# A four-layer graph network on one core: two VectorE operations read PSUM, one block changes from multiplying to gathering, one group of steps is timed by the count alone

## The chip, the cores and the metric

The kernel runs on one core of a Trainium2 chip. The metric is the device time of one execution in microseconds; of several executions the median is given, with the lowest and the highest. The engines are called as the profile calls them: PE (TensorE matmul), PEld (its weight load), DVE (VectorE), ACT (ScalarE), POOL (GpSimd) and SP (SyncE, which here issues DMAs only).

## The reference, cut to what matters

There are 6250 nodes with 256 channels each and 100,000 edges, sorted by destination. Each of four layers adds to every node the sum of the rows of its sources and sends the result through three small matrix products; the fourth layer is the head, whose middle width is 64.

```python
def agg(h):
    return jax.ops.segment_sum(h[src], dst, num_segments=N)
for l in range(NL - 1):
    h = x + agg(x)
    h = jax.nn.relu(h @ W1s[l] + b1s[l])
    h = jax.nn.relu(h @ W2s[l] + b2s[l])
    x = h @ W3s[l] + b3s[l]
h = x + agg(x)
h = jax.nn.relu(h @ cW1 + cb1)
h = jax.nn.relu(h @ cW2 + cb2)
return h @ cW3 + cb3
# called with h = max(layernorm(x), 0); the result is added to x
```

Everything is float32. The layer norm and the last addition to x are a small part of the time.

## The kernel before, in words

**Blocks.** The nodes are cut into 49 blocks of 128 destinations. The rows of all nodes stay in SBUF as a tile `XY` of 128 x 49 x 512: for each block 256 channels of a rounded high part and 256 of the rest, so that two fast passes make a float32 product. The same rows lie in DRAM as `table0` to `table3`, one per layer.

**Two ways to aggregate.** A destination block is either multiplied or gathered.

- Multiplied: a matrix of edge counts, 128 destinations against all 6250 sources, is multiplied with `XY`. That is 49 matmuls named `agg`: line 1797 in layer 0, where the block's counts have just been built, and line 1880 in layers 1 to 3 for groups of four blocks (line 1797 again for a block that stands alone). The counts themselves are built in layer 0 by matmuls named `bp` (line 1202) from one-hots named `hi` and `lo` (DVE, line 1164), cast to bytes (lines 1210 and 1212) and written to DRAM for the later layers.
- Gathered: POOL issues 16 indirect DMAs (sometimes one more, named `over`), each bringing the rows of 128 edges from the table (line 1557). PE then adds them into one PSUM tile `sums` with narrow one-hot matrices `hot` (23 matmuls, 46 records in the profile, line 1620). This is called a visit. `hot` is made by DVE on line 1601 by comparing the column numbers `colf` with the destinations `rel`. DVE then adds the block's own rows: `u` from the two halves of `XY` (line 1641, issued at once after the visit's matmuls), and three steps later `u + sums` (line 1650).

**After the aggregation** both ways go on alike: transposes (line 1681, named a turn), a relu into `h1`, then what the code calls seconds (line 1379: the second matrix product) and thirds (line 1442: the third; in the head lines 1371 and 1391, with line 1439 for a piece of the end). Their outputs become the next layer's `XY` and table. A block's old rows in `XY` may be overwritten once all uses are marked in a set named `used`.

**Which block goes which way.** Layer 0 gathers 24 blocks (0 to 18 and 44 to 48) and multiplies 25 (19 to 43; block 19 comes first, alone). Layers 1, 2 and 3 gather 21, 20 and 19 and multiply the rest.

**The order of the work** is written out when the program is built, by a planner that counts two things: `now`, one tick for each unit of (usually) four `agg` matmuls, and `clock`, an estimate of PE's time. `Gathered.flow` sends gathers at an even pace over a layer by the estimate; each gather is tied to the PE matmul after which it was sent (`after(...)`, which becomes a semaphore wait on POOL). `Gathered.meets` says when a visit is due: when the estimate has reached it, or a fixed number of ticks before the layer's end (`LATE`), and not sooner than four ticks after the visit before. A visit that is due sends whatever of its gathers is not yet sent. Turns wait in a list `jobs`, seconds and thirds in a list `queue`, each with a first and a last tick; between the two they are placed at the next visit, and at the last tick at any rate (the stretch is `SPAN`, six ticks). `step` (line 1262 on) keeps the entries of `queue` a few ticks apart (`free`). The group of the last gathered block of a layer, block 48, is marked `hurry` and has no such stretch; the group gathered just before it (44 to 47 in layer 0, blocks from 16 on in later layers) has one like all the others.

Of the kernel before, what the change touches and what calls it, by code (L numbers as in the profile page):

```python
# [8 lines left out]
F32 = mybir.dt.float32  # L9
# [5 lines left out]
OP = mybir.AluOpType  # L15
PSUM = bass.MemoryType.PSUM
DRAM = bass.MemoryType.DRAM
P = 128
# [378 lines left out]
def sorted_edges(  # L397
# [38 lines left out]
    nc = tc.nc  # L436
    N, C = x.shape
# [16 lines left out]
    Q = P // 4  # L454
    T = 16
# [14 lines left out]
    gone = [(0, 4), (4, 4), (8, 4), (12, 4), (16, 4), (44, 4), (48, 1)]  # L470
    panels = [(20, 4), (24, 4), (28, 4), (32, 4), (36, 4), (40, 4), (44, 4)]
    solos = [[], [], [19], [18, 19]]
# [2 lines left out]
    S0 = 2 * min(place_of)  # L475


    teams = [(19, 1), (20, 4), (24, 4), (28, 4), (32, 4), (36, 4), (40, 2), (42, 2)]
    made = [b + i for b, n in teams for i in range(n)]
    for i in range(panels[-1][1]):  # L480
        made.insert((4, 9, 14, 18)[i], panels[-1][0] + i)
    made.insert(23, 18)
    assert sorted(made) == sorted(place_of) and sum(gone[-3]) == panels[0][0] and gone[-2] == panels[-1] and all(n == gone[0][1] for _, n in gone[:-1]) and sorted(
        b + i for b, n in gone[:-2] + gone[-1:] + panels for i in range(n)) == list(range(NT))
    NQ = len(gone)
# [2 lines left out]
    left = [T * sum(n for _, n in gone[:q]) for q in range(NQ + 1)]  # L488
# [15 lines left out]
    XY = const.tile([P, NT, 2 * C], F32R, name="XY")  # L504
# [581 lines left out]
    with tc.manual_schedule():  # L1086
# [167 lines left out]
        def step(visit):  # L1254

            g = queue[0]
            rush = any(o["hurry"] for o in queue)
            first, last = g["first"], g["last"]
            if rush:
                first = min(first, g["since"] + 3)  # L1260
            if now[0] < max(first, free[0]) or not (visit or last <= now[0] or rush):
                return
            g["steps"].pop(0)()
            lock[0] = now[0] + (1 if g["hurry"] else 2)
            free[0] = now[0] + (2 if g["hurry"] else 3 if rush else 4)
            g["since"] = now[0]
            if g["steps"]:
                g["first"], g["last"] = now[0] + g["far"], now[0] + g["far"] + SPAN
            else:
                queue.pop(0)  # L1270

# [30 lines left out]
        def reload(l, j):  # L1302

            if (l, j) in used and (l, j) in kept and l < NLAYER:
                wanted.append((l, j))
                bring()
# [39 lines left out]

            later(2, biased)

        def mlp(l, b0, n, h1, hurry, far):

            w = n * P
            end = l == NLAYER
# [124 lines left out]
            def thirds():  # L1477
# [4 lines left out]
                for i in range(0, n, 2):  # L1482
                    third(i)

            wait = 1 if hurry else far - 2
            queue.append(dict(steps=[seconds, thirds], since=now[0], first=now[0] + wait,
                              last=now[0] + wait + (0 if hurry else SPAN),
                              far=2 if hurry else far, hurry=hurry))


        class Gathered:
            def __init__(self, l):
                self.l, self.sent, self.done = l, 0, 0
                self.first, self.rest, self.turns = None, 0, []
                b0, n0 = teams[0] if l == 0 else panels[-1]
                others = solos[l] + [b0 + i for i in range(n0)]
                self.blocks = [(b, n if l or b != gone[-3][0] else n - teams[0][1], i,
                                left[q] + i * T)
                               for q, (b, n) in enumerate(gone) for i in range(n)
                               if b + i not in others]  # L1500
                self.alone = {b + i for b, n, i, _ in self.blocks}
                self.visits = [(g, rounds) for g in range(len(self.blocks)) for rounds in ROUNDS]
                self.n = len(self.visits)
                self.rows, self.us, self.hots = {}, [], -1

                self.order, self.upto, self.shared = [], [0], {}
                seen_over = set()
                for g, rounds in self.visits:
                    b = self.blocks[g][0] + self.blocks[g][2]
                    new = [T] if over_of[b] not in seen_over else []  # L1510
                    seen_over.add(over_of[b])
                    used_at = {k: i for i, c in reversed([*enumerate(rounds)])
                               for k in range(c, T + 1, 4) if k in (*range(own[b]), *new)}
# [70 lines left out]
            def one_hots(self, v):  # L1584
                if self.hots >= v:
                    return
                self.hots = v
                g, rounds = self.visits[v]
                which = over_of[self.blocks[g][0] + self.blocks[g][2]]
                if which not in known:  # L1590
                    known.add(which)
                    m = P // Q - 1
                    c = T - 4 * m - min(rounds)
                    for b in over[which]:
                        nc.vector.tensor_scalar(
                            rel[:, list(own).index(b), 0, c, m:m + 1],
                            late_dst[:, which:which + 1], float(-b * P), None,
                            op0=OP.add)
                shape = [P, len(rounds), P // Q, Q]
                self.hot = work.tile(shape, F32, name="hot")  # L1600
                nc.vector.tensor_tensor(
                    self.hot,
                    colf.rearrange("p (m q) -> p m q", q=Q)[:, None, :, :].to_broadcast(shape),
                    rel[:, self.blocks[g][3] // T, v % len(ROUNDS), :, :, None].to_broadcast(shape),
                    OP.is_equal)

# [31 lines left out]
            def finish(self, b, n, g, sums):  # L1638
                u = work.tile([P, C], F32, name="u", bufs=2)
                self.us.append(u)  # L1640
                nc.vector.tensor_tensor(u, XY[:, b + g, :C].bitcast(F32),
                                        XY[:, b + g, C:].bitcast(F32), OP.add)
                used.add((self.l, b + g, 0))
                if (self.l, b + g, 1) in used:
                    used.add((self.l, b + g))
                    reload(self.l, b + g)
                behind = []
                later(1, lambda: behind.extend(paced))
                later(1 if b == gone[-1][0] else 3, lambda: after(
                    nc.vector.tensor_tensor(u, u, sums[:, :C], OP.add),  # L1650
                    "a full product stands behind the sums", behind))

                self.closed(b, n, g)

            def closed(self, b, n, g):
                if g % 2 or g == n - 1:
                    us, self.us = self.us, []

                    def turn():
                        if g < 2:  # L1660
                            self.h1 = work.tile([P, KC, W], F32, name="h1", bufs=2)
                        turned(self.l, us, self.h1, g)
                        if g == n - 1:
                            mlp(self.l, b, n, self.h1, b == gone[-1][0], far)

                    far = FAR - 2 if b == self.blocks[-2][0] else FAR
                    if b == gone[-1][0]:
                        later(2, turn)
                    else:
                        job(far - 2, far - 2 + SPAN, turn)  # L1670
                        self.turns.append(jobs[-1])
                if g + 1 < n and (self.l, b + g + 1) in alone:
                    self.us.append(alone.pop((self.l, b + g + 1)))
                    self.closed(b, n, g + 1)
# [31 lines left out]
        alone = {}  # L1706
        spare = clT.rearrange("p a q s -> p (a q s)").bitcast(F32)
        sums = ps_g.tile([P, W], F32, name="sums")
        MARGIN = 6.0
        TAIL = [16.0] + [-5.0] * (NLAYER - 1) + [-3.0]  # L1710
        LATE = [-8] + [10] * (NLAYER - 1) + [-5]
# [294 lines left out]
```

## Time and profile before

| | |
|---|---|
| median of 3 runs | 2053.34 us (2052.33 to 2054.1) |
| profiled execution | 2053.2 us, its span 2051.3 us, granted clock 0.994 |
| PE busy | 1997.9 us, 97% of the span |
| POOL busy | 1416.9 us, 69%; 1336 `rows` gathers of 0.991 us on average |
| DVE, ACT busy | 45%, 42% |
| preparation before layer 0's products | to about 105 us |
| layer 0, 1, 2, 3 (with the end) | to about 661, 1155, 1619, 2051 us |

The profiled execution spends 1.9 us outside its span. A row of the groups reads: line, engine, operation, output and inputs, how often; then busy time and mean duration, and the engine's idle time just before, with what ended it. A row of the timeline reads: start, duration, engine, line, operation, and in brackets the idle time before it and its releaser.

### The profile page before, as it was taken

To read this page: it belongs to the slowest core of one execution; us is meant where nothing else is said; L and a number is where in the kernel's file an instruction comes from. 1 tells how busy PE (TensorE), PEld (TensorE's weight loads), DVE (VectorE), ACT (ScalarE), POOL (GpSimd) and SP (SyncE) were. 2 spreads that over 40 slices of the span, in tenths; PEclk is the share of its full clock that TensorE was granted. 3 is DMA by queue.
4 is the path that set the end of the run, shared out by engine and by line. 5 is a ranking of instruction groups with operands and counts; after the bars stand their busy time and mean duration, and the time that the engine had idled before them with its cause. 6 is when DMAs were issued, how large, how long until landed. Compare 5 with 4: busy or idle time off the path is not lost.

```text
span 2051.3 us, 33099 instructions
## 1 busy us (share of the span) xinstructions
PE 1997.9 (97%) x12078; PEld 1480.8 (72%) x12078; DVE 912.8 (45%) x2093; ACT 853.5 (42%) x1746; POOL 1416.9 (69%) x1460
## 2 busy tenths in 40 slices
PE   6999999999999999999999999999999999999997
PEld 5767666666767777777777777777777777777675
DVE  6888776676662422222334322222234332333333
ACT  5776655555555533322233433323334433323231
POOL 4657777777774477777777377777777277777773
PEclk9999999999999999999999999999999999999999
DMA  6544555454455655555556554455456455665554
GB/s 198 163 137 151 156 148 160 152 155 151 147 158 172 213 165 156 156 178 156 167 171 205 172 162 151 148 171 174 140 180 212 147 183 167 202 195 190 175 155 129
DMA packets 182290, 341.84 MB, mean 167 GB/s; under 512 B 31588, under 2 KB 117108, under 8 KB 182118
## 3 DMA queue, kind: packets, MB, share of 16 engines
q0 software_dynamic: 67376, 181.01, 30.0%
q1 hardware_dynamic: 112566, 156.54, 23.2%
q10 hardware_dynamic: 2176, 2.10, 0.3%
q8 instruction: 96, 1.57, 0.3%
q14 instruction: 76, 0.62, 0.1%
HBM read 282.26 MB, written 57.26 MB: 166 GB/s over the span
## 4 chain that ended last, share of the span: by engine, by line
PE 90%; DVE 3%; DMA 3%; issue 1%; ACT 1%; POOL 1%; SPq 0%; DVEq 0%; ACTq 0%; POOLq 0%
PE agg L1880 46%; PE agg L1797 14%; PE sums L1620 10%; PE ps L1442 6%; PE ps L1379 6%; PE bp L1202 4%; DMA rows<-table,idx 2%; PE ps L1681 1%; DVE hi L1164 1%; DVE at L1212 1%; PE ps L1391 1%; DVE lo L1164 1%; PE ps L1371 0%; PE bp L1030 0%; DMA wd<-in_dst_dram,starts 0%
## 5 line engine op out<-in xcount | busy, mean ns | idle before, releaser
L1557 POOL DMA_INDIRECT rows<-table,idx x1336 | 1323.6, 991 | 559.5 <-issue 227.1
L1880 PE MATMUL agg<-a,XY 128*128 128x512 f32 x4116 | 977.9, 395 | 2.0 <-ACT a L1773 2.0
L1880 PEld LDWEIGHTS agg<-a,XY 128*128 128x128 f32 x4116 | 766.0, 188 | 190.9 <-issue 33.0
L1773 ACT CAST a<-at 128x512 fp32r<-128x512 uint8 (+1 forms) x536 | 325.3, 618 | 622.5 <-PE agg L1880 591.7
L1773 DVE CAST a<-at 128x512 fp32r<-128x512 uint8 x535 | 243.9, 458 | 498.1 <-PE agg L1880 471.5
L1797 PE MATMUL agg<-XY,a 128*128 128x512 f32 x1372 | 380.9, 410 | 1.4 <-ACT a L1757 0.7
L1797 PEld LDWEIGHTS agg<-XY,a 128*128 128x128 f32 x1372 | 241.1, 190 | 44.6 <-issue 5.4
L1620 PE MATMUL sums<-rows,hot 128*32 128x256 f32 x3680 | 240.7, 381 | 9.8 <-DMA rows<-table,idx 9.7
L1620 PEld LDWEIGHTS sums<-rows,hot 128*32 128x32 f32 x3680 | 121.6, 110 | 122.9 <-issue 31.5
L1210 ACT CAST at<-bp 128x392 uint8<-128x392 f32 x250 | 121.0, 489 | 197.0 <-PE bp L1202 196.4
L1757 ACT CAST a<-at 128x512 fp32r<-128x512 uint8 (+2 forms) x349 | 190.7, 575 | 6.6 <-PE agg L1797 6.2
L1212 DVE CAST at<-bp 128x392 uint8<-128x392 f32 x230 | 129.4, 563 | 137.0 <-PE bp L1202 136.7
L1650 DVE TENSOR_TENSOR u<-u,sums 128x256 f32<-128x256 f32 x84 | 35.2, 420 | 282.1 <-PE agg L1880 265.1
L1164 DVE TENSOR_TENSOR hi<-cols,pairs 128x784 bf16<-128x784 bf16 x240 | 134.5, 561 | 0.0
L1442 PE MATMUL ps<-w,h 128*128 128x256 f32 x588 | 133.6, 379 | 0.9 <-ACT h L1382 0.9
L1379 PE MATMUL ps<-h,w 128*128 128x512 f32 (+3 forms) x328 | 133.1, 548 | 0.3 <-ACT h L1893 0.3
L1202 PE MATMUL bp<-hi,lo 128*128 128x196 bf16 x960 | 125.9, 252 | 6.3 <-DVE hi L1164 5.7
L1202 PEld LDWEIGHTS <-lo 128*128 128x128 bf16 x960 | 70.9, 98 | 75.1 <-issue 26.0
L1442 PEld LDWEIGHTS ps<-w,h 128*128 128x128 f32 x588 | 111.5, 190 | 17.6 <-ACT h L1382 1.3
L1164 DVE TENSOR_TENSOR lo<-lanes,pairs 128x512 bf16<-128x512 bf16 x240 | 99.9, 416 | 2.7 <-ACT pairs L1159 1.5
L1379 PEld LDWEIGHTS ps<-h,w 128*128 128x128 f32 x328 | 60.0, 190 | 53.9 <-issue 42.9
L1450 DVE TENSOR_TENSOR zz<-ps,w 128x512 f32<-128x512 f32 (+1 forms) x76 | 50.3, 672 | 107.4 <-PE ps L1442 107.4
(214 smaller groups left out, 1041.6 us busy)
## 6 DMA issues: line engine op xcount, KB each, us to landing
at<-mat SPq DMA_DIRECT2D x150, 448.0 KB
mat<-at SPq DMA_DIRECT2D x30, 784.0 KB
rows<-table,idx POOLq DMA_INDIRECT x1336
table<-zz SPq DMA_DIRECT2D x71, 256.0 KB
back<-table SPq DMA_DIRECT2D x95, 128.0 KB
xs<-in_x_dram SPq DMA_DIRECT2D x8, 768.0 KB
table<-zs SPq DMA_DIRECT2D x12, 512.0 KB
out_dram<-zz SPq DMA_DIRECT2D x23, 256.0 KB
```

The costliest lines, as they stand in the source:

```text
L1164: nc.vector.tensor_tensor(o.rearrange("p q (n t) -> p q n t", t=2), values.rearrange("p (n t) -> p n t", t=2)[:, None, :, :].to_broadcast( ...
L1202: mm = nc.tensor.matmul(bp[:, m * HW:(m + 1) * HW], lo[:, q + m, :], hi[:, q + m, :], start=True, stop=True)
L1210: nc.scalar.copy(o, v)
L1212: nc.vector.tensor_copy(o, v)
L1379: mm = nc.tensor.matmul(ps[:mp, :w], weights[l][0][:, c, i * P:i * P + mp], h1[:, c, :w], start=(c == 0), stop=(c == KC - 1))
L1442: mm = nc.tensor.matmul(o, h2[0][:, c, nodes], w3[:, c, :], start=(c == 0), stop=(c == KC - 1))
L1557: got = nc.gpsimd.indirect_dma_start(out=t, out_offset=None, in_=tables[self.l][:, :], in_offset=bass.IndirectOffsetOnAxis(ap=at, axis=0),)
L1620: nc.tensor.matmul(self.sums[m * Q:(m + 1) * Q, :C], self.hot[:, c - min(rounds), m, :], self.shared[over_of[b + i]] if k == T else self.r ...
L1757: nc.scalar.copy(a[:, i * m * P:(i + 1) * m * P].rearrange("p (j d) -> p j d", j=m), counts[b][:, j:j + m, :])
L1773: cast(o, at[:, :, d:d + m * P])
L1797: mm = nc.tensor.matmul(agg, a[:, d:d + P], XY[:, j, :], start=(j == 0), stop=(j == NT - 1))
L1880: mm = nc.tensor.matmul(agg[c][:, :w], XY[:, j, o:o + P], a[:, :w], start=(at == 0 and half == 0), stop=(at == NT - 1 and half == 1))
```

## The change

Three things are changed together.

1. **PSUM operands.** `colf` is copied once into a part of the PSUM tile `sums` that the visits do not use, and the comparison that makes `hot` reads it there. The own rows are added in two steps that each read one operand in PSUM: first the low half of `XY` onto `sums` in place, then `sums` plus the high half into `u`. Both now come after the visit, where before only the second did, and the mark in `used` moves to the second.
2. **The group before the last.** It is marked `brisk`: its turn is placed four ticks after its visit, seconds two ticks later, thirds three ticks after those, without a stretch. `step` keeps two ticks after a step while a `hurry` group is queued (three before), and three after a brisk one (four before).
3. **25 and 24.** In layer 0 block 19 is now gathered, in the group of 16 to 19. Its counts are still built, since layers 2 and 3 use them, but as the 26th block instead of the first.

```diff
-    teams = [(19, 1), (20, 4), (24, 4), (28, 4), (32, 4), (36, 4), (40, 2), (42, 2)]
+    teams = [(20, 4), (24, 4), (28, 4), (32, 4), (36, 4), (40, 2), (42, 2)]
...
-    made.insert(23, 18)
+    for i, b in ((23, 18), (25, 19)):
+        made.insert(i, b)
...
-            free[0] = now[0] + (2 if g["hurry"] else 3 if rush else 4)
+            free[0] = now[0] + (2 if g["hurry"] or rush else 3 if g["brisk"] else 4)
             g["since"] = now[0]
             if g["steps"]:
-                g["first"], g["last"] = now[0] + g["far"], now[0] + g["far"] + SPAN
+                g["first"], g["last"] = now[0] + g["far"], now[0] + g["far"] + (0 if g["brisk"] else SPAN)
...
-            wait = 1 if hurry else far - 2
+            wait = 1 if hurry else 2 if brisk else far - 2
             queue.append(dict(steps=[seconds, thirds], since=now[0], first=now[0] + wait,
-                              last=now[0] + wait + (0 if hurry else SPAN),
-                              far=2 if hurry else far, hurry=hurry))
+                              last=now[0] + wait + (0 if hurry or brisk else SPAN),
+                              far=2 if hurry else far, hurry=hurry, brisk=brisk))
...
-                    colf.rearrange("p (m q) -> p m q", q=Q)[:, None, :, :].to_broadcast(shape),
+                    sums[:, C:C + P].rearrange("p (m q) -> p m q", q=Q)[:, None, :, :].to_broadcast(shape),
...
-                nc.vector.tensor_tensor(u, XY[:, b + g, :C].bitcast(F32),
-                                        XY[:, b + g, C:].bitcast(F32), OP.add)
-                used.add((self.l, b + g, 0))
-                if (self.l, b + g, 1) in used:
-                    used.add((self.l, b + g))
-                    reload(self.l, b + g)
                 behind = []
+
+                def whole():
+                    after(nc.vector.tensor_tensor(sums[:, :C], sums[:, :C],
+                                                  XY[:, b + g, C:].bitcast(F32), OP.add),
+                          "a full product stands behind the sums", behind)
+                    nc.vector.tensor_tensor(u, sums[:, :C], XY[:, b + g, :C].bitcast(F32), OP.add)
+                    used.add((self.l, b + g, 0))
+                    if (self.l, b + g, 1) in used:
+                        used.add((self.l, b + g))
+                        reload(self.l, b + g)
+
                 later(1, lambda: behind.extend(paced))
-                later(1 if b == gone[-1][0] else 3, lambda: after(
-                    nc.vector.tensor_tensor(u, u, sums[:, :C], OP.add),
-                    "a full product stands behind the sums", behind))
+                later(1 if b == gone[-1][0] else 3, whole)
...
-                    far = FAR - 2 if b == self.blocks[-2][0] else FAR
+                    brisk = b == self.blocks[-2][0]
+                    far = 3 if brisk else FAR
...
-                        job(far - 2, far - 2 + SPAN, turn)
+                        wait = 4 if brisk else far - 2
+                        job(wait, wait + (0 if brisk else SPAN), turn)
...
         sums = ps_g.tile([P, W], F32, name="sums")
+        nc.vector.tensor_copy(sums[:, C:C + P], colf)
```

Over the whole program PE has 49 `agg` matmuls of layer 0 fewer and 23 `sums` matmuls more; POOL has 16 rows more; the stretches of `agg` matmuls begin 30 times fewer right after `bp` matmuls (200 instead of 230). In the changed file line 1797 is 1803, 1880 is 1886, 1681 is 1686, 1442 is 1443, 1379 is 1380, 1371 is 1372 and 1391 is 1392. The rest of the order is mostly the old one. Three places where it moves follow.

**PE where layer 0 ends and layer 1 begins.** `agg<-XY,a` is layer 0's product, `agg<-a,XY` layer 1's, `ps<-w,h` are thirds and `ps<-h,w` seconds of gathered groups. Before:

```order
L1442 MATMUL ps<-w_1185,h_8205 128x256 x4
L1797 MATMUL agg<-XY,a 128x512 x12
L1379 MATMUL ps<-h_7705,w_1183 128x512 x4
L1797 MATMUL agg<-XY,a 128x512 x6
L1880 MATMUL agg<-a,XY 128x512 x4
L1442 MATMUL ps<-w_1185,h_8313 128x256 x8
L1880 MATMUL agg<-a,XY 128x512 x8
```

After the change:

```order
L1443 MATMUL ps<-w_1186,h_8170 128x256 x4
L1803 MATMUL agg<-XY,a 128x512 x8
L1380 MATMUL ps<-h_7662,w_1184 128x512 x4
L1803 MATMUL agg<-XY,a 128x512 x10
L1443 MATMUL ps<-w_1186,h_8270 128x256 x8
L1886 MATMUL agg<-a,XY 128x512 x8
```

The eight thirds that stood behind layer 1's first four products now stand ahead of them.

**PE at the kernel's end**, around the last visit of the head (the rows of line 1620). Before:

```order
L1391 MATMUL ps<-clT,h_20172 128x256 x4
L1880 MATMUL agg<-a,XY 128x512 x8
L1681 MATMUL ps<-ident,u 128x128 x4
L1681 MATMUL ps<-ident,us 128x128 x2
L1681 MATMUL ps<-ident,clT 128x128 x2
L1880 MATMUL agg<-a,XY 128x512 x4
L1620 MATMUL sums<-rows,hot 32x256 x17
L1620 MATMUL sums<-over,hot 32x256
L1620 MATMUL sums<-rows,hot 32x256 x3
L1880 MATMUL agg<-a,XY 128x512 x8
```

After the change (the first row is the end of the visit before the last):

```order
L1620 MATMUL sums<-rows,hot 32x256 x4
L1886 MATMUL agg<-a,XY 128x512 x16
L1686 MATMUL ps<-ident,u 128x128 x4
L1686 MATMUL ps<-ident,us 128x128 x2
L1686 MATMUL ps<-ident,clT 128x128 x2
L1620 MATMUL sums<-rows,hot 32x256 x17
L1620 MATMUL sums<-over,hot 32x256
L1620 MATMUL sums<-rows,hot 32x256 x3
L1886 MATMUL agg<-a,XY 128x512 x8
```

The last visit now comes 16 products and eight transposes behind the one before it (before, 44 products stood between the two), and 12 products are left behind it instead of 24.

**POOL, the last eight gathers of the program**, with the semaphores that each waits for (`PE_49` is a wait for a PE matmul, `DMASW` one for a DMA queue's slot). Before:

```order
L1557 DMA rows_20250<-table3_90,idx_74 128x256 [waits DMASW6_49]
L1557 DMA rows_20254<-table3_90,idx_74 128x256 [waits DMASW7_49,PE_49]
L1557 DMA rows_20266<-table3_90,idx_74 128x256 [waits DMASW0_49,PE_49]
L1557 DMA rows_20277<-table3_90,idx_74 128x256 [waits DMASW1_49,PE_49]
L1557 DMA over_20291<-table3_90,late_src_76 128x256 [waits DMASW2_49,PE_49]
L1557 DMA rows_20301<-table3_90,idx_74 128x256 [waits DMASW3_49,PE_49]
L1557 DMA rows_20313<-table3_90,idx_74 128x256 [waits DMASW4_49,PE_49]
L1557 DMA rows_20325<-table3_90,idx_74 128x256 [waits DMASW5_49,PE_49]
```

After the change:

```order
L1557 DMA rows_20290<-table3_90,idx_74 128x256 [waits DMASW6_49,PE_49]
L1557 DMA rows_20300<-table3_90,idx_74 128x256 [waits DMASW7_49,PE_49]
L1557 DMA rows_20310<-table3_90,idx_74 128x256 [waits DMASW0_49,PE_49]
L1557 DMA rows_20329<-table3_90,idx_74 128x256 [waits DMASW1_49]
L1557 DMA over_20331<-table3_90,late_src_76 128x256 [waits DMASW2_49]
L1557 DMA rows_20333<-table3_90,idx_74 128x256 [waits DMASW3_49]
L1557 DMA rows_20335<-table3_90,idx_74 128x256 [waits DMASW4_49]
L1557 DMA rows_20337<-table3_90,idx_74 128x256 [waits DMASW5_49]
```

Before, each of the last seven waits for a PE matmul of its own, spread over the products ahead of the visit. Now the last five have no such wait: they stand right behind `rows_20310`, which is tied to the last product ahead of the eight transposes.

More of the change, by code (lines that the diff above doesn't have):

```diff
@@ L1347, in bring_inputs, with mlp @@
             later(2, biased)
-        def mlp(l, b0, n, h1, hurry, far):
+        def mlp(l, b0, n, h1, hurry, far, brisk=False):
             w = n * P
@@ L1494, in __init__ @@
                 self.first, self.rest, self.turns = None, 0, []
[L1495 to L1498, printed above, removed]
+                b0, n0 = panels[-1]
+                others = solos[l] + [b0 + i for i in range(n0) if l]
+                self.blocks = [(b, n, i, left[q] + i * T)
                                for q, (b, n) in enumerate(gone) for i in range(n)
@@ L1663, in turn @@
                         if g == n - 1:
-                            mlp(self.l, b, n, self.h1, b == gone[-1][0], far)
-                    far = FAR - 2 if b == self.blocks[-2][0] else FAR
+                            mlp(self.l, b, n, self.h1, b == gone[-1][0], far, brisk)
+                    brisk = b == self.blocks[-2][0]
+                    far = 3 if brisk else FAR
                     if b == gone[-1][0]:
```

## The prediction, made before the changed kernel ran

> **What bounds the kernel now.** I read the page first, then the windows by stage, the waits of PE's rows in each stage, the instructions of the gather's line, and the timeline at four places.
>
> ```profile
> PE 1997.9 (97%) x12078; PEld 1480.8 (72%) x12078; DVE 912.8 (45%) x2093; ACT 853.5 (42%) x1746; POOL 1416.9 (69%) x1460
> 105.00:661.00 556.00, 544.12 (x3672) 382.80 (x3673) 383.32 (x903) 331.38 (x771) 400.78 (x401) 0.99 0.51 153
> 661.00:1155.00 494.00, 490.75 (x2805) 369.52 (x2804) 163.30 (x350) 170.93 (x326) 336.90 (x340) 1.00 0.55 172
> 1155.00:1619.00 464.00, 464.00 (x2650) 348.98 (x2649) 142.92 (x301) 152.75 (x275) 317.90 (x324) 1.00 0.54 166
> 1619.00:2051.30 432.30, 418.05 (x2535) 312.42 (x2533) 142.59 (x297) 129.54 (x232) 303.86 (x308) 0.99 0.56 177
> ```
>
> The columns of a window are its length, then busy time and count of PE, PEld, DVE, ACT and POOL, the granted clock, the DMA share and GB/s. PE is full in layers 1 and 2 (494 against 490.8, 464 against 464.0), so there only PE's work counts. In layer 0 it stands still 11.9 us, and in the last stage 14.3. What it waits for there, window 105 to 650 first, then 1620 to 2052 (total us, times, longest):
>
> ```profile
> PEld sums L1620 <- DMA rows<-table,idx: 9.5, 9, 2.5
> PE sums L1620 <- DMA rows<-table,idx: 5.9, 6, 2.0
> ...
> PEld sums L1620 <- DMA rows<-table,idx: 6.2, 5, 2.7
> PE sums L1620 <- DMA rows<-table,idx: 3.8, 3, 2.2
> ```
>
> So visits wait for gathered rows: 9.5 us in layer 0, 6.2 in the head, by the weight loads, which come first. The gathers' own line in layer 0:
>
> ```profile
> L1557 POOL DMA_INDIRECT rows<-table,idx x382 | 382.2, 1001 | 142.7 <-issue 64.9 <-PE agg L1797 27.0 <-PE bp L1202 25.2
> L1557 POOL DMA_INDIRECT rows<-table,idx x382: 940/947/1622, 105.8 to 642.4; - x191
> 120.00:150.00 30.00, 17.21 (x17) 1.00 0.41 124
> 150.00:250.00 100.00, 98.84 (x689) 69.73 (x688) 80.56 (x192) 66.52 (x154) 75.09 (x76) 1.00 0.49 147
> 250.00:350.00 100.00, 98.61 (x687) 69.16 (x686) 69.18 (x162) 54.97 (x125) 76.81 (x77) 1.00 0.53 157
> ```
>
> (The third row holds the gather's line alone.) POOL shows 77% busy, yet it is full: between two gathers lie 0.30 us in which it issues (timeline below), and 77 in 100 us are one per 1.30. The median gather lasts 0.947 us, the mean 1.001. Layer 0 is thus a race between PE and POOL, and at its visits POOL ends last. I count everything against that: an edit that frees PE there only lengthens its waits, one that frees POOL shortens them.
>
> **What beside them lengthens gathers.** The first, one typical and the last of 23 pairs in layer 0, each a comparison `hot` and the gather with which it overlaps most; between the two typical rows lies a `u + sums` with a PSUM operand:
>
> ```profile
> 151.48 0.96 POOL L1557 DMA_INDIRECT rows<-table,idx  x1 [0.30 <-PE agg L1797]
> 151.53 0.95 DVE L1601 TENSOR_TENSOR hot<-colf,rel 128x768 f32<-128x768 f32 x1
> ...
> 302.04 0.98 POOL L1557 DMA_INDIRECT rows<-table,idx  x1 [0.30 <-issue]
> 302.11 0.41 DVE L1650 TENSOR_TENSOR u<-u,sums 128x256 f32<-128x256 f32 x1
> 303.02 0.95 DVE L1601 TENSOR_TENSOR hot<-colf,rel 128x768 f32<-128x768 f32 x1
> 303.32 1.47 POOL L1557 DMA_INDIRECT rows<-table,idx  x1 [0.30 <-issue]
> ...
> 634.03 0.95 DVE L1601 TENSOR_TENSOR hot<-colf,rel 128x768 f32<-128x768 f32 x1
> 634.58 1.23 POOL L1557 DMA_INDIRECT rows<-table,idx  x1 [0.30 <-PE agg L1797]
> ...
> 142.79 0.99 POOL L1557 DMA_INDIRECT rows<-table,idx  x1 [0.31 <-PE agg L1797]
> 143.36 0.42 DVE L1641 TENSOR_TENSOR u<-XY 128x256 f32<-128x256 f32 x1
> ```
>
> Beside a `hot`, both of whose operands lie in SBUF, a gather takes up to 0.52 us more than the median; beside the PSUM form (302.11) it takes 0.98. Over all of layer 0 the excess is 6.2 us for 24 comparisons (0.26 each) and 3.1 us for 24 own rows of line 1641 (0.13 each; the last two rows are the first). For this the Trainium skill has two rules on its page "SBUF — State Buffer", section "Who interferes with whom", and they disagree about this change. One says that a DVE instruction with two SBUF inputs contends with a GpSimd instruction that reads SBUF, and one with a single SBUF input does not. The other infers that `tensor_tensor` does not hold up descriptor generation, since it takes only the read interface of the shared pair. By the second rule the relief below would be nothing; the 1.47 us stand against it, and I let the rows decide.
>
> **The change, part by part.**
>
> *POOL in layer 0.* One more block is 16 gathers: 16 x 1.30 = **+20.8**. The new operands give back 25 x (0.26 + 0.13) = **−9.7**; bounds: nothing, and all that the mean stands above the median, 389 gathers (with the seven `over`) x 0.054 = 21.0. POOL also waits at gates that PE opens: of the 142.7 us idle, 382 x 0.30 = 115 are issuing, some 28 are gates, and from 120 to 150 it issues only 17 instead of 23. PE reaches the gates earlier, by at most what it saves before them (8.5, next item). I take **−3**, a third; bounds 0 and −8.5. POOL, and with it the end of layer 0: +20.8 − 9.7 − 3 = **+8.1**.
>
> *PE in layer 0.* A product less and a visit more:
>
> ```profile
> 621.73 4.62 PE L1797 MATMUL agg<-XY,a 128*128 128x512 f32 x19 [0.69 <-DVE un L1809]
> 659.57 1.94 PE L1797 MATMUL agg<-XY,a 128*128 128x512 f32 x6
> 663.51 1.17 PE L1880 MATMUL agg<-a,XY 128*128 128x512 f32 x4 [2.00 <-ACT a L1773]
> 664.51 3.62 PE L1442 MATMUL ps<-w,h 128*128 128x256 f32 x16
> 1965.84 2.73 PE sums L1620 x46
> ```
>
> 19 products from 621.73 to 626.19 are 0.235 us each: −49 x 0.235 = −11.5; a visit without waits is 2.73 (last row, from the chain that ends with it) and some 0.3 of edges: +3.0. PE alone gains 8.5. As POOL ends 8.1 later, these 8.5 turn into waits: 9.5 + 8.5 + 8.1 = 26 us of waits at layer 0's visits. The term on the path is POOL's, not PE's.
>
> *Layer 0 to layer 1.* Layer 1's first product waits 2.00 us for its cast. After the change the 16 records of thirds (3.62 us) that stood behind it stand ahead: the wait is covered, **−2.0** (bounds 0 and −2.0). If that cover is gone it costs the 2.0 again.
>
> *Layers 1 and 2.* No waits before; PE's work is equal. The own rows come three ticks later, but `u + sums` already did; the second pass is another 0.42 us of an engine that is a third busy. **0**. Late marks in `used` delay reloads of `XY`, which have a layer of time.
>
> *The head's visits.* 6.2 us of waits, of them 2.4 at the last visit. The others come from the same race, with 0.39 us relief per visit for waits of 3.8 in all: **−2.5** (bounds 0, −3.8).
>
> *The last visit.* The rows where it now waits:
>
> ```profile
> 2022.15 0.89 PE ps L1681 x8
> 2023.04 0.20 issue
> 2023.24 5.16 DMA rows<-table,idx
> 2028.41 0.04 issue
> 2028.45 0.62 PE sums L1620 x2
> ```
>
> This is the chain of waits: the last gather began 0.64 us ahead of the visit (2023.88), landed 5.16 later, and two matmuls closed the visit at 2029.07. In the changed order the gathers for it are tied more tightly: one to the first of only 16 products ahead of the transposes, the next with no wait of its own, then three through those products, and five behind the last of these. With 16 x 0.235 + 0.89 = 4.65 us from the first of these products to the visit, and 1.25 per gather (0.95 + 0.30), the first starts at best 4.3 ahead and the tenth, nine later, 7.0 behind the visit's start. It lands at 7.0 + 5.16 = 12.2, the visit is over at 12.8 instead of 2029.07 − 2023.88 = 5.2: **+7** (rounded down, since a gather's landing beside less traffic may be shorter). Bounds: 0, if landing and gates turn out as before; +9, if POOL has a backlog of two gathers there. What follows it, 12 products and the last group's chain, needs the same time; the own rows' extra 0.42 hides behind the 8 products of 2 us.
>
> Sum: +8.1 − 2.0 + 0 − 2.5 + 7 = **+10.6** on 2053.2, the profiled execution's own time, which is the median of the runs shown within 0.2: **2063.8**, and I write 2064.
>
> **Rivals.**
>
> *A: the late gathers at the end do not bite.* For: if PE loses a few us anywhere in the 20 us before, POOL catches up, and a landing of 5.16 may be a long one. Against: five gathers without a wait of their own cannot start before the one ahead of them. The end is +8.1 − 2.0 − 2.5 = +3.6: 2056.8.
>
> *B: no relief on POOL.* The excess beside `hot` might come from the DMA traffic of the same moment, or a PSUM operand might hold the port just as long. For: 23 pairs have excesses from 0.01 to 0.52. Against: the short ones overlap little. +9.7 more: 2073.5. (By the second rule of the Trainium skill's page "SBUF — State Buffer", section "Who interferes with whom", the time would be this one.)
>
> *C: POOL is freed so far that PE sets layer 0.* The mechanism is the same relief, only larger: every gather falls to 0.947, because DVE's hold-ups also reach gathers that do not overlap them. Its place is layer 0, its price 21.0 instead of 9.7, and POOL's gates (8.5) then open as early as PE comes: 20.8 − 21.0 − 8.5 = −8.7, and PE's own gain of 8.5 shows in full. It decides where relief and earlier gates together reach 20.8 + 8.5 = 29.3, nearly all of both; less by 4.1 us than before the total is from 27 on. −8.5 − 2.0 − 2.5 + 7 = −6.0: 2047.2. For: the 54 ns are there, and so are 28 us at gates. Against: half of them are counted beside other work (the `hi` and `lo` one-hots, which stay).
>
> *D: a count-timed step stands in PE's queue before its input.* A brisk group's turn now comes four ticks after its visit, 4 x 4 x 0.235 = 3.8 us, seconds two ticks later (1.9 us), with nothing to move it. `u` needs a tied pass and two DVE operations of 0.42; where DVE is 70 to 80% busy (layer 0) a wait of 1 us at two or three steps would follow: forecast +3, 2067.
>
> **How the numbers follow.** What a measurement of this kernel can tell from no change is about 0.2%, 4.1 us: faster is below 2049.2, slower above 2057.4. Chances: forecast 0.42 (2059 to 2069), A 0.18, B 0.12, C 0.12, D 0.08; the rest, 0.08, is what I have not thought of, half of it faster. Slower: forecast, B, D, a third of A and some of the rest, 0.70. Same: the rest of A, and C where it falls a little short, 0.18. Faster: C and half of the rest, 0.12. The range takes in A and most of B and leaves C out: 2052 to 2073.
>
> **What would show it.** Right: gathers beside `hot` and own rows at 0.95 in the rows of line 1557, their mean in layer 0 near 0.976; waits of `sums` for `rows` in layer 0 at 20 us or more, layer 0's last visit about 8 us later; no 2.00 wait ahead of layer 1's first product; one wait of 8 us or more at the head's last visit, with the last gather issued some 7 us after that visit began. Wrong: gathers still at 1.2 to 1.5 beside `hot` (B); waits below 10 us in layer 0 (C); a last visit under 7 us (A); new waits of PE at lines 1686 or 1380 (D).

## The result, and the profile after

The changed kernel takes 2080.06 us (median, 2078.07 to 2080.62) where the kernel before takes 2053.07 in the same session: a ratio of 1.0132, with a 95% interval of 1.012 to 1.0145. It is slower, as forecast, but by 27.0 us and not by 10.6, and the time lies above the range. The profiled execution has a span of 2078.8 us.

The windows by stage of the changed kernel (length; busy time and count of PE, PEld, DVE, ACT and POOL; clock, DMA share, GB/s):

```profile
105.00:690.00 585.00, 544.58 (x3668) 376.92 (x3669) 387.19 (x907) 330.13 (x757) 408.25 (x417) 0.99 0.50 150
690.00:1165.00 475.00, 474.19 (x2724) 355.24 (x2723) 155.51 (x331) 163.49 (x307) 330.00 (x340) 1.00 0.56 174
1165.00:1640.00 475.00, 473.85 (x2697) 356.55 (x2696) 148.32 (x310) 154.31 (x285) 314.85 (x324) 1.00 0.53 163
1640.00:2078.80 438.80, 424.85 (x2561) 317.08 (x2559) 147.12 (x306) 134.52 (x238) 299.38 (x308) 0.99 0.56 177
```

Layer 0 now ends near 690 instead of 661, and in it PE is idle 40.4 us instead of 11.9. The later stages are as full as before. So the loss is layer 0's: its last visit starts at 672.5 instead of 645.3, 27.2 us later, and the end of the span is 27.5 us later.

What PE waits for in layer 0 of the changed kernel, weight loads first, then matmuls (total us, times, longest; window 105 to 660):

```profile
PEld L1203 <- DVE hi L1165: 68.8, 111, 1.7
PEld L1203 <- DVE at L1213: 11.7, 42, 0.5
...
PE bp L1203 <- DVE hi L1165: 35.8, 57, 2.8
```

The rows for `hi` of the kernel before (window 105 to 650):

```profile
PEld L1202 <- DVE hi L1164: 21.8, 63, 1.0
PE bp L1202 <- DVE hi L1164: 5.7, 9, 2.8
```

There is no row of `sums` waiting for `rows` any more; before, weight loads waited 9.5 us there and matmuls 5.9. What has grown instead is the wait for DVE's `hi` one-hots, at the building of the counts: from 21.8 to 68.8 us for weight loads and from 5.7 to 35.8 for matmuls. All 25 visits of layer 0 take 2.73 us. The race between PE and POOL that the prediction described does not take place, since a third engine, DVE, is later than both.

The timeline of the changed kernel's PE and DVE at the end of a visit and behind it shows how (start, duration, engine, line, operation, idle before and releaser):

```profile
430.03 0.68 PE L1203 MATMUL bp<-hi,lo 128*128 128x196 bf16 x6
430.49 1.18 PE L1803 MATMUL agg<-XY,a 128*128 128x512 f32 x4
430.63 0.57 DVE L1213 CAST at<-bp 128x392 uint8<-128x392 f32 x1 [9.18 <-issue]
431.12 0.41 DVE L1165 TENSOR_TENSOR lo<-lanes,pairs 128x512 bf16<-128x512 bf16 x1
431.45 0.56 DVE L1165 TENSOR_TENSOR hi<-cols,pairs 128x784 bf16<-128x784 bf16 x1
...
433.38 0.51 PE L1203 MATMUL bp<-hi,lo 128*128 128x196 bf16 x4
433.69 0.41 DVE L1165 TENSOR_TENSOR lo<-lanes,pairs 128x512 bf16<-128x512 bf16 x1
434.02 0.56 DVE L1165 TENSOR_TENSOR hi<-cols,pairs 128x784 bf16<-128x784 bf16 x1
434.50 0.56 DVE L1213 CAST at<-bp 128x392 uint8<-128x392 f32 x1
434.63 0.34 PE L1203 MATMUL bp<-hi,lo 128*128 128x196 bf16 x2 [0.74 <-DVE hi L1165]
434.76 0.48 PE L1803 MATMUL agg<-XY,a 128*128 128x512 f32 x1
```

DVE stands idle for 9.18 us before 430.63, because no counts are built in that stretch; from 430 on six `bp` matmuls stand between four products, and DVE, without a gap from there on, makes its `lo`, `hi` and cast in 1.28 us for every four of them. In the built order the reason can be counted. Before the change, 228 runs of `bp` matmuls in layer 0 have four and one has six. After it, 130 have four and 65 have six, with stretches of up to 32 products without any between them (before, up to 8). That follows from the planner: it may build counts only while one of three buffers is free, the places of the six blocks that layer 0 builds but does not multiply decide when one comes free, and what is late is then built at up to six matmuls a tick.

The other steps, in the changed kernel's rows. First the gathers of layer 0, all and beside a `hot`, then the chain at the head's last visit:

```profile
L1557 POOL DMA_INDIRECT rows<-table,idx x381 | 372.8, 979 | 157.9 <-issue 65.6 <-PE agg L1803 34.4 <-PE bp L1203 33.9
...
416.45 0.95 DVE L1601 TENSOR_TENSOR hot<-sums,rel 128x768 f32<-128x768 f32 x1
416.67 0.95 POOL L1557 DMA_INDIRECT rows<-table,idx  x1 [0.30 <-issue]
...
2051.20 0.95 POOL over L1557
2052.52 1.18 issue
2053.70 0.95 POOL rows L1557
2054.95 2.69 DMA rows<-table,idx
2057.69 1.06 PE sums L1620 x2
```

The gathers are relieved as forecast: their mean is 979 ns instead of 1001 (0.976 was written), the excess of those beside a `hot` falls from 6.2 us to 0.4, and that beside an own row from 3.1 us to 0.5. What is left lies in gathers that also overlap a `hi` or `lo` one-hot: of the 29 gathers beside a `hot` or an own row and no such one-hot, none exceeds 0.946 us by more than 10 ns (before the change, such gathers did by up to 0.45 us). The last visit begins at 2047.4, its last gather is issued at 2054.95, 7.5 us later, and the visit takes 11.23 us instead of 5.12.

### The profile page after: what moved, and what is told of

Its sections match the earlier page's. It is cut to its first block, busy times and chain, and to the rows that moved or that the text cites. A ratio compares the mean times of both kernels' runs of the same rounds, so it can differ in the third digit from the quotient of the medians.

```text
span 2078.8 us, 33002 instructions
## 1 busy us (share of the span) xinstructions
PE 1998.8 (96%) x12067; PEld 1473.0 (71%) x12067; DVE 919.0 (44%) x2096; ACT 851.4 (41%) x1727; POOL 1410.0 (68%) x1476
## 4 chain that ended last, share of the span: by engine, by line
PE 86%; DVE 9%; issue 2%; ACT 1%; DMA 1%; POOL 0%; SPq 0%; DVEq 0%; POOLq 0%; ACTq 0%
PE agg L1886 45%; PE agg L1803 11%; PE sums L1620 11%; PE ps L1443 6%; PE ps L1380 6%; PE bp L1203 3%; DVE hi L1165 2%; DVE at L1213 2%; DVE lo L1165 1%; PE ps L1686 1%; PE bp L1031 1%; PE ps L1372 1%; PE ps L1392 1%; DVE hot L1601 0%; DMA near_i<-in_dst_dram,at_i 0%
## 5 line engine op out<-in xcount | busy, mean ns | idle before, releaser
L1779 ACT CAST a<-at 128x512 fp32r<-128x512 uint8 x535 | 325.9, 619 | 605.4 <-PE agg L1886 574.1
L1779 DVE CAST a<-at 128x512 fp32r<-128x512 uint8 (+1 forms) x536 | 242.7, 455 | 504.5 <-PE agg L1886 475.5
L1803 PE MATMUL agg<-XY,a 128*128 128x512 f32 x1323 | 366.2, 411 | 0.7 <-ACT a L1763 0.7
L1803 PEld LDWEIGHTS agg<-XY,a 128*128 128x128 f32 x1323 | 235.6, 190 | 46.1 <-issue 7.4
L1763 ACT CAST a<-at 128x512 fp32r<-128x512 uint8 (+2 forms) x336 | 183.1, 572 | 28.0 <-PE agg L1803 27.5
L1644 DVE TENSOR_TENSOR sums<-sums,XY 128x256 f32<-128x256 f32 x85 | 36.5, 430 | 301.1 <-PE agg L1886 277.6
L1203 PE MATMUL bp<-hi,lo 128*128 128x196 bf16 x960 | 128.1, 253 | 38.3 <-DVE hi L1165 35.8
L1203 PEld LDWEIGHTS <-lo 128*128 128x128 bf16 x960 | 69.8, 99 | 112.2 <-DVE hi L1165 68.8
L1380 PE MATMUL ps<-h,w 128*128 128x512 f32 (+2 forms) x320 | 133.1, 558 | 0.8 <-ACT h L1690 0.5
L1690 ACT ACTIVATE h<-ps,bias 128x256 f32<-128x256 f32 (+1 forms) x116 | 47.8, 465 | 158.1 <-PE ps L1686 157.9
```

Source lines behind the costliest of these rows:

```text
L1203: mm = nc.tensor.matmul(bp[:, m * HW:(m + 1) * HW], lo[:, q + m, :], hi[:, q + m, :], start=True, stop=True)
L1380: mm = nc.tensor.matmul(ps[:mp, :w], weights[l][0][:, c, i * P:i * P + mp], h1[:, c, :w], start=(c == 0), stop=(c == KC - 1))
L1763: nc.scalar.copy(a[:, i * m * P:(i + 1) * m * P].rearrange("p (j d) -> p j d", j=m), counts[b][:, j:j + m, :])
L1779: cast(o, at[:, :, d:d + m * P])
L1803: mm = nc.tensor.matmul(agg, a[:, d:d + P], XY[:, j, :], start=(j == 0), stop=(j == NT - 1))
```

## The experiments

Three theories stood at the start. Theory 1: the bursts of building, which come with the third part of the change. Theory 2: the own rows' two passes, both behind the visit in DVE's queue, hold up the one-hots behind them (first part). Theory 3: the steps placed by count (second part).

**e1_spread: the bursts taken away.** Only the places of the six blocks in the building order differ from the changed kernel.

```diff
-        made.insert((4, 9, 14, 18)[i], panels[-1][0] + i)
-    for i, b in ((23, 18), (25, 19)):
+        made.insert((3, 8, 12, 16)[i], panels[-1][0] + i)
+    for i, b in ((20, 18), (24, 19)):
```

> The changed kernel, with only the places in the building order altered at which the six blocks stand whose counts layer 0 does not multiply (3, 8, 12, 16, 20, 24 instead of 4, 9, 14, 18, 23, 25). In the built order the ticks with six bp matmuls fall from 65 to 7. Theory 1 (bursts of building: the three count buffers stop the building, and what is then caught up at six matmuls a tick asks more one-hots of DVE than it makes): PE's weight loads wait for hi one-hots about 20 us in layer 0 instead of 68.8, as before the change, visits of layer 0 wait for rows again (up to 15 us), total 2050 to 2064. Theory 2 (the own rows' two passes, both behind the visit in DVE's queue, hold up the one-hots behind them) and theory 3 (the steps placed by count hold PE or ACT): the waits for hi stay above 55 us, total 2075 to 2083.

Measured: 2060.31 us (2058.93 to 2062.84), ratio 1.0041 (1.0025 to 1.0058). Six places in the building order take back about 20 us. The waits of weight loads for `hi` are 43.3 us, not 20, so theory 1 holds for the larger part, and something of DVE's shortage remains without bursts. Visits of layer 0 wait 6.1 us again.

**e2_psum, e3_brisk, e4_move: each part alone on the kernel before.** Their diffs are the three parts of the change.

> The kernel before with the PSUM operands alone. Theory 1: no bursts here (228 ticks of four bp matmuls as before); gathers beside hot at 0.95 us, waits of layer 0's visits for rows fall from 9.5 to under 4 us, the head's from 6.2 to under 3: 2044 to 2050. Theory 2: waits for hi above 50 us, 2070 or more. Theory 3: as before, within 3 us of 2053.

> The kernel before with the brisk group alone. Theory 1: layer 0 as before, the 2.0 us wait at layer 1's first product gone, and at the head's last visit a wait of some 8 us instead of 2.4, since the built order ties the last five gathers behind the last product ahead of it: 2055 to 2061. Theory 2: the same. Theory 3 (the steps placed by count cost layer 0 its 27 us): 2075 or more.

> The kernel before with block 19 moved from multiplying to gathering alone, operands and group as before. Theory 1: the bursts are here (65 ticks of six bp matmuls), so waits for hi of 60 us or more in layer 0, and since the gathers are not relieved visits may wait on top: 2072 to 2085. Theories 2 and 3: no waits for hi beyond 25 us; POOL ends later by 16 gathers, 2060 to 2072.

| | time, us | ratio to before (95%) | layer 0: PEld waits for hi, us | layer 0: visits over 2.73, us | head's last visit, us |
|---|---|---|---|---|---|
| before | 2052.6 | | 21.8 | 9.4 | 5.12 |
| e2_psum | 2046.01 | 0.9966 (0.9954 to 0.9978) | 28.3 | 1.4 | 5.77 |
| e3_brisk | 2052.89 | 1.0006 (0.9993 to 1.0019) | 20.9 | 9.0 | 11.39 |
| e4_move | 2079.25 | 1.0132 (1.0117 to 1.0148) | 67.7 | 6.4 | 6.26 |
| the change | 2080.06 | 1.0132 (1.012 to 1.0145) | 68.8 | 0.0 | 11.23 |

Theories 2 and 3 fall: the first part alone is faster by 0.34%, the second makes no difference that can be told. The move alone costs all that the change costs, with the same wait for `hi`. The parts do not add up (by the ratios −7, +1 and +27 against +27). The rows fit one reason: where PE waits 68 us for DVE, a relieved POOL takes the 6.4 us at visits away and layer 0 ends no sooner for it (its last visit starts at 670.5 in e4_move and at 672.5 in the change). For e3_brisk the expectation was 2055 to 2061. Its late last visit is there (11.39), so it wins some 5 us elsewhere; where is open. The 2.0 us wait ahead of layer 1's first product, which I expected the brisk group to cover, stays in e3_brisk, now put down to another releaser:

```profile
PE agg L1882 <- DMA table<-zz: 2.0, 1, 2.0
```

The cover asks for the second and the third part together: e5b_nomove, further below, which lacks the third, keeps the 2.0 us, and e4_move, which has the third alone, waits 1.9 at the same place.

**e7b_casts: more of DVE's time in the bursts.** The changed kernel, with its order of PE.

```diff
-                    if step % 2 or step <= 2 * PRE:
+                    if step % 4 or step <= 2 * PRE:
                         nc.scalar.copy(o, v)
```

> The changed kernel, where in layer 0 DVE makes every fourth of the casts of line 1213 instead of every second, and ACT the others; the order of PE is the same, with 65 ticks of six bp matmuls. If in these bursts DVE has too little time (a pair of bp matmuls asks 0.64 us of it, 1.28 for the usual four, which come with four products in 1.30 us; six ask 1.9 in about 1.5), a cast of 0.56 less for every eight bp matmuls shortens them: PE's weight loads wait for hi under 40 us in layer 0 instead of 68.8, total 2060 to 2070. Rival: the bursts wait on the chain from one-hot to matmul to buffer, not on DVE's time, or ACT (half busy) becomes as late: waits for hi or for the casts stay above 55 us together, total 2075 or more.

Measured: 2070.05 us (2068.33 to 2070.8), ratio 1.0083 (1.0067 to 1.0098); `hi` waits 45.6 us. So DVE's time is what the bursts lack: 0.5% comes back with not a matmul moved. The trace of the changed kernel speaks against the rival, a chain through the buffers: of the 68.8 us of waits for `hi`, 67.0 fall where DVE stands idle for less than 0.2 us in all during the wait and the microsecond ahead of it, so the one-hots are late while DVE is at work. The relief is less than expected: the waits stay above 40 us, and the time is at the upper edge of its range. Visits wait 6.2 us again, since the gathers lengthen. A likely reason, not tested by itself, is that with fewer casts between them the `lo` and `hi` one-hots lie closer together. The gathers of this kernel in layer 0:

```profile
L1557 POOL DMA_INDIRECT rows<-table,idx x389 | 388.9, 1000 | 143.7 <-issue 62.5 <-PE agg L1803 31.7 <-PE bp L1203 26.6
```

1000 ns on average, where the changed kernel has 979.

**e5b_nomove and e8b_nomove_tail13: the change without its third part, and then with the head's gathers ending earlier.** The first undoes the third part; the second has in addition:

```diff
-        TAIL = [16.0] + [-5.0] * (NLAYER - 1) + [-3.0]
+        TAIL = [16.0] + [-5.0] * (NLAYER - 1) + [13.0]
```

> The changed kernel without its third part: PSUM operands and the brisk group, with 24 blocks gathered and 25 multiplied as before. If the parts add up: e2_psum's layer 0, no 2.0 us wait ahead of layer 1's first product, and the late gathers at the head's last visit (a wait of about 8 us, where e2_psum has 3.0): 2043 to 2049. If the brisk group only pays where POOL is relieved: under 2042.

> e5b_nomove with the head's gathers planned to end earlier (the last entry of TAIL 13 instead of -3): the last gather is tied 30 products ahead of the last visit instead of none. If the late gathers cost what the wait shows, the last visit takes under 5 us instead of some 11 and the total is 5 to 8 us below e5b_nomove. Rival: POOL, full, ends them no earlier, and the waits only move to the visits before: within 2 us of e5b_nomove.

Measured: e5b_nomove 2051.45 us, ratio 0.9993 (0.9984 to 1.0003), its last visit 11.32 us; e8b_nomove_tail13 2041.85 us (2039.48 to 2042.88), ratio 0.9947 (0.9933 to 0.996), its last visit 2.72 us. The late gathers at the end cost what the wait shows, and a little more than the 5 to 8 us expected: 9.6 us between the two, 8.6 of them in that visit. The parts do not quite add up in e5b_nomove, which came out 2.5 us above the window. e8b_nomove_tail13 beats the kernel before by 0.53% and the change by 1.8%.

**e12_all and e13_spread_tail13: can the 25th gathered block pay?** Both are the whole change with the spread building order of e1_spread and the head's last TAIL entry at 13; e12_all also has the casts of e7b_casts.

> The whole change with three repairs: the six blocks spread in the building order (as e1_spread), DVE with a quarter of the casts (as e7b_casts), the head's gathers ending earlier (as e8b_nomove_tail13). If DVE's shortage in layer 0 was all that spoiled the 25th gathered block, this is below e8b_nomove_tail13 by PE's 8.5 us or a part of it. If POOL's 16 gathers more bound layer 0 once DVE no longer does, its visits wait 10 us or more for rows and it stays 4 to 15 us above e8b_nomove_tail13: 2045 to 2055.

> e1_spread with the head's gathers planned to end earlier (the last entry of TAIL 13 instead of -3), DVE's casts as in the change. If e1_spread's excess over the kernel before is the last visit's wait of 8 us, the total falls by 8 to 10 us as it did from e5b_nomove to e8b_nomove_tail13: 2049 to 2053, and against e8b_nomove_tail13 the 25th gathered block costs 8 to 11 us more than it saves. If layer 0 holds the excess in waits that the tail does not touch: 2056 or more.

Measured: e13_spread_tail13 2051.38 us, ratio 0.9999 (0.9988 to 1.001), inside its window; e12_all 2060.91 us, ratio 1.0036 (1.0022 to 1.005). The only difference of e13_spread_tail13 from e8b_nomove_tail13 is block 19 with the building order that it asks for, and it costs 9.5 us by the medians, 10.7 by the ratios, each to the kernel before in its own session. What PE waits for in layer 0, weight loads, in e8b_nomove_tail13, in e13_spread_tail13 and in e12_all:

```profile
PEld L1202 <- DVE hi L1164: 28.1, 71, 1.5
```

```profile
PEld L1203 <- DVE hi L1165: 42.7, 81, 1.7
...
PEld sums L1620 <- DMA rows<-table,idx: 8.1, 10, 2.2
```

```profile
PEld sums L1620 <- DMA rows<-table,idx: 22.4, 25, 2.5
PEld L1203 <- DVE hi L1165: 19.8, 44, 1.4
```

Without bursts the block adds 14.6 us of waits for DVE and some 6 us at visits (7.1 over 2.73 each instead of 1.3), against 8.5 us of PE's work saved. With DVE unloaded, e12_all, the wait for `hi` is as before the change, and then the visits wait, 24.6 us by their durations. That is POOL as the bound, as the second case of its expectation said, but the time is above its window. Its gathers take 1007 ns on average, where e13_spread_tail13, which differs in the casts alone, has 983; 24 ns on each of some 390 gathers are 9 us, an estimate that fits the difference. The same edit that gained 10 us amid bursts (e7b_casts) loses 9.5 without them (7.6 by the ratios).

**e10b_psum_tail1: the earlier end without the brisk group.**

> e2_psum with the last entry of TAIL 1 instead of -3: the last gather is tied 24 products ahead of the last visit instead of 10. The last visit's wait of 3.0 us goes: 2042 to 2045 where e2_psum had 2046. Rival: the visits before it wait instead, as POOL is full: 2046 or more.

Measured: 2044.58 us, ratio 0.9968 (0.9957 to 0.9979), against e2_psum's 0.9966. The last visit's wait is gone (2.72 us), but the visits of the head ahead of it are 1.5 us over 2.73 each in sum, and 0.2 in e2_psum. Between gain and rival it stays undecided.

**A disturbed session.** e5_nomove, e7_casts, e8_nomove_tail13 and e10_psum_tail1 are the same kernels as those with a b. They ran first, in a session in which the kernel before itself took 2334.89 us; their ratios there were 0.9952 (0.9929 to 0.9975), 1.0103 (1.0057 to 1.0149), 0.993 (0.9909 to 0.9952) and 1.0004 (0.9983 to 1.0026). The order among them is the same but for e10; the sizes are not used.

## Why the prediction was wrong, step by step

- **POOL and PE in layer 0, the step that failed.** I wrote that layer 0 is a race between PE and POOL, and that PE's saving of 8.5 us turns into waits at visits: 26 us of them, with the layer's end 8.1 us later. Measured: no wait at visits, the last visit 27.2 us later, and 47 us of new waits of weight loads (68.8 − 21.8) at the building of the counts. With the 9.4 us of waits at visits and the 8.5 us of work that went, 47.0 − 9.4 − 8.5 = 29.1 us account for the delay, roughly, since weight loads overlap matmuls. I had read DVE as 70 to 80% busy and not as a bound. Of the waits of layer 0 I showed those of `sums` alone, 9.5 us for weight loads and 5.9 for matmuls; the wait for `hi` in the same answers, 21.8 and 5.7, was the larger or as large, and had no term in the sum. One steady cycle of the kernel before shows the bound. Two runs of four `bp` matmuls with four products between them, and DVE's operations of that cycle:

```profile
308.87 0.51 PE L1202 MATMUL bp<-hi,lo 128*128 128x196 bf16 x4
308.92 0.56 DVE L1164 TENSOR_TENSOR hi<-cols,pairs 128x784 bf16<-128x784 bf16 x1
309.16 1.17 PE L1797 MATMUL agg<-XY,a 128*128 128x512 f32 x4
309.42 0.57 DVE L1212 CAST at<-bp 128x392 uint8<-128x392 f32 x1
309.90 0.42 DVE L1164 TENSOR_TENSOR lo<-lanes,pairs 128x512 bf16<-128x512 bf16 x1
310.17 0.52 PE L1202 MATMUL bp<-hi,lo 128*128 128x196 bf16 x4
310.24 0.56 DVE L1164 TENSOR_TENSOR hi<-cols,pairs 128x784 bf16<-128x784 bf16 x1
```

PE's cycle is 1.30 us; DVE's, from `hi` to `hi`, is 1.32 here and 1.28 in the burst above, with no gap in it. DVE keeps up only because some ticks have no building in them. Taking away a block's product takes away 13 ticks (49 matmuls at four a tick), not only work of PE; that would explain the 14.6 us of waits for DVE that e13_spread_tail13 has over e8b_nomove_tail13, but its building order differs too, and the two were not separated.
- **The count that I quoted and did not read.** The stretches of products that begin right after `bp` matmuls fell from 230 to 200 for the same 960 `bp` records. I left this out of the sum. It was the sign of the bursts, which cost about 20 of the 27 us (from the change to e1_spread: 2080.06 to 2060.31 by the medians, 18.7 by the ratios).
- **The relief of the gathers** was right in kind and nearly in size: 9.7 us were written; the excess beside `hot` and own rows fell from 9.3 us to 0.9 in the change and to 2.3 in e2_psum, and e2_psum is 6.6 us faster than the kernel before. Rival B falls. The rest of the excess, 12 us before and after, lies beside the `lo` and `hi` one-hots, which stay, as the argument against rival C said.
- **Rival C.** The sign that was named for it, waits below 10 us at layer 0's visits, is there (0.0 us), and its mechanism is not: the mean gather takes 979 ns and not 947, and layer 0 ends later, not sooner. The sign fits any cause that delays PE by more than POOL, and so could not tell C from what happened.
- **POOL as the bound of layer 0 with 25 blocks** was right where DVE does not come first: in e12_all the visits wait 24.6 us, where 26 were forecast. That agreement is in part luck, since there the gathers are longer than I reckoned.
- **Layer 0 to layer 1:** the 2.0 us wait is gone in the changed kernel, as written.
- **Layers 1 and 2:** 0 was written; layer 1's last visit is 27.9 us later and layer 2's 25.3, against 27.2 for layer 0's, so 1.9 us were won on the way. Which step they come from is open.
- **The head:** the waits at its other visits, 3.6 us, are gone (−2.5 was written). The last visit takes 6.1 us more (+7 was written), and rival A falls. The last gather was issued 7.5 us behind the visit's start, where 7.0 had been worked out, and landed in 2.7 us instead of 5.16; the step is right and a little smaller than its working.
- **Rival D**, a step placed by count that stands in PE's queue before its input, falls too. In layer 0 of the changed kernel PE waits 2.0 us in two waits at line 1686 for ACT, which is the sign that was named for it; but both lie before transposes of multiplied blocks (`un`), and e4_move, which has no brisk group, has the same two, 1.42 and 0.57 us. e3_brisk shows no loss.

With the bursts gone, e1_spread stands 7.7 us above the kernel before, where 10.6 had been forecast; but its layer 0 is made of other waits than I wrote, 43.3 us for DVE and 6.1 at visits.

## What to carry to other kernels

Before an engine is called a bound or not, reckon one steady cycle of each engine, not its share of a window: here DVE, at some 70% of layer 0, was full in the cycles with building that are shown and caught up in those without. When a change takes work off the longest engine, ask which other engine used that work as its time to catch up, and count in the built order how the remaining work is spread, since the same work in stops and bursts, in place of an even rate, cost some 20 us here. A planner's list of places that fits one order has to be fitted again when an item leaves it.

## What the runs showed of the hardware that was not expected

- A gather's length follows what lies beside it on DVE, and no other cause was found: in layer 0 of nine of these kernels the 67 to 114 gathers with no DVE operation beside them have a mean excess over 0.946 us of no more than 1 ns. In the kernel before, the five beside a two-SBUF `hot` and no other such operation have 0.29 us on average and up to 0.45. The Trainium skill's page "SBUF — State Buffer", section "Who interferes with whom", infers that a `tensor_tensor` does not hold up descriptor generation; these runs show that a float32 one with two SBUF inputs does, and that one input in PSUM ends it (at most 3 ns for the 13 gathers beside such a `hot` alone in the changed kernel). For the bf16 one-hots, beside which the rest of the excess lies, no run changed the operands.
- Taking other work off DVE made the gathers longer, not shorter: with a quarter of the casts on DVE the mean rose from 979 (the change) to 1000 ns (e7b_casts), and from 983 (e13_spread_tail13) to 1007 (e12_all).
- In the disturbed session PE stood still at places that have no releaser in the profile, at a mean granted clock of 0.98 instead of 0.995. Two waits of weight loads over the whole of e5_nomove there, and below them those of e5b_nomove, the same kernel in an undisturbed session:

```profile
PEld sums L1620 <- issue: 173.4, 276, 2.0
PEld L1202 <- issue: 93.5, 171, 4.7
```

```profile
PEld sums L1620 <- issue: 30.3, 74, 0.8
PEld L1202 <- issue: 26.2, 80, 2.6
```

What caused it is open.
